# A two-layer graph attention and expert kernel: the rows of five pairs fetched and normalized during layer 0's last expert blocks, and one ring of single-row buffers beside attention 1

## The chip, the cores and the metric

The kernel runs on one core of a Trainium2 chip. The core has a tensor engine (PE, with a second row PEld for its weight loads), a vector engine (DVE), a scalar engine (ACT), a general engine (POOL) and SyncE (SP), whose queue issues most of the DMAs here. All of them work through their own instructions in order and wait for one another with semaphores. The metric is the time of one execution in microseconds on the device, lower is better. Line numbers (L1444) are those of the kernel before.

## The reference

N = 2708 nodes with 256 features, and a 0/1 adjacency matrix of 2708 x 2708. Two layers, each a graph attention and a sparse mixture of experts, with residuals:

```python
# layer 0
x = x + gnn0(layernorm(x), adj)       # h = x W^T; softmax over neighbours of leaky_relu(s_i + s_j); att @ h
x = x + ffn0(layernorm(x))            # 8 experts, top 2, 256 -> 1024 -> 256, erf gelu
# layer 1
x = x + gnn1(layernorm(x), adj)       # hyperbolic: logmap, W_gcn, expmap/logmap, W_att, masked softmax,
                                      # elu, proj, logmap, sigmoid, expmap
x = x + ffn1(layernorm(x))            # 16 experts, top 2, 256 -> 512 -> 256, relu, then y = layernorm(x + moe)
```

All data is float32. What matters here is the seam between the two layers: attention 1 of any node needs `layernorm(x)` of all nodes, where x is the finished output of layer 0, and its projection `u = layernorm(x) @ w1x` (two weight matrices of 256 x 256 side by side, so 512 columns) must be there for all nodes before any row of attention 1 can be summed.

## The kernel before

**Tiles.** The nodes are cut into T = 22 tiles of up to 128 rows (20 full ones and two of 74 rows), taken as 11 pairs. `x_all` holds x of all tiles while layer 0's attention runs; `h_all` holds 22 x 257 values per partition in layer 1.

**Layer 0's experts.** The router scatters every node's row (twice, top 2) to pages of 128 rows per expert in DRAM (`rows_d`). 47 sure blocks and three that run only if needed (`rest`, behind a branch at L929) then go through `Experts.run`: for block b, SP loads W1 and W2 of its expert (1 MB each, L743 and L747) two blocks ahead into one of three rooms, and fetches the 128 rows three blocks ahead (L759). PE multiplies `hid_ps` (L874), ACT applies gelu with the table loaded for it (L878), PE multiplies `out_ps` of the block before (L892), DVE scales it (L898, after `side` at L866 and the weight `w`, ACT L868), and POOL adds the rows with an indirect DMA into one of two sums in DRAM, `sums0[0]` for even blocks and `sums0[1]` for odd ones (L903). `sums0[0]` begins with x, so x of layer 1 is `sums0[0] + sums0[1]`. A hook `beside(b)` is called in every block after its row fetch.

**The seam.** After the branch of `rest`, ACT loads another table (L1418). Then `project1` is started for one pair after another by `Turns`, a list of generators that are stepped round by round: this only writes down the order of instructions on each engine; the engines then run as their waits allow. A pair goes through: two fetches of 256 KB from the sums (L1444), POOL's sum of the two (L1468), a store of the sum to `x_d` in DRAM (L1455), DVE's mean and variance (L421, L422), ACT's Ln and Exp for the deviation (L428, L429), one Newton step on DVE (L374), two normalizations (L437) into tiles `xr`, four transposes on PE (L455), ACT's copy `xts` (L1491) and sums of squares (L1496), eight matmuls `u_ps` (L460), and for each tile a sum of squares and a copy to `h_all` on ACT (L1505, L1507). The fetch of the first pair has to wait until the last add of layer 0 has landed, and the PE has nothing else to do. `factors1` then makes the softmax factors, `split_h` the two halves of h, and attention 1 begins (L1570). POOL widens the masks (L1430, two of them ahead of the first pair; ACT widens two, L1432).

**Attention 1 and layer 1's experts** are ordered by a planner: generators tell what engine they want and for how long, and `Clock` and `Slots` order them. `points1` closes a group of six tiles: it fetches its x back from `x_d`, three pairs into the ring `xp` of four pair buffers (`xps`, four slots), combines them on DVE (L1778), normalizes on ACT and gives the rows to the router. The same SP queue then carries the weights and rows of layer 1's experts.

**Buffers.** Pools stand on one another in SBUF; a pool that is opened where another was closed makes its first writer wait for the last reader there.

**DMA semaphores.** The built program gives SP's transfers eight semaphores in turn, so a transfer is issued only once the one eight places ahead of it has landed.

Of the kernel before, what the change touches and what calls it, by code (L numbers as in the profile page):

```python
# [22 lines left out]
P = 128  # L23
# [123 lines left out]
def kernel(  # L147
# [72 lines left out]
    def row_tile(name, bufs):  # L220
        return row.tile([P, D], F32, name=name, tag=name, bufs=bufs)
# [26 lines left out]

    room_scope = ExitStack()
# [6 lines left out]
    def xn_tile():  # L256
        return keep0.tile([P, RW], F32, name="xn", bufs=4)
# [16 lines left out]

    x_all = keep0.tile([P, T, D], F32, name="x_all")
# [431 lines left out]
    class Experts:  # L707
# [5 lines left out]
        def __init__(self, layer, router, w1, b1, w2, func, sums, tags, xg, xt, bias, sure):  # L713
            self.layer, self.router, self.w1, self.w2 = layer, router, w1, w2
            self.func, self.sums, self.b1 = func, sums, b1
            self.t_tag, self.h_tag, self.o_tag = tags
            self.xg_tile, self.xt_tile, self.bias_tile = xg, xt, bias
            E, _, self.F = w1.shape
            self.FC, self.NB = self.F // P, router.blocks
            self.rooms, self.rows, self.known, self.planned, self.stages = {}, {}, 0, 0, []  # L720
            self.last_add, self.adds = {}, []
            self.b1_rows = w1x.rearrange("p c f -> p (c f)")[:E, :self.F]
            self.taken, self.sure = taken_of[layer], sure
# [177 lines left out]
        def add(self, b, yo):  # L901
            k = b % 2
            ins = nc.gpsimd.indirect_dma_start(  # L903
                out=self.sums[k][:, :], in_=yo, in_offset=None,
                out_offset=bass.IndirectOffsetOnAxis(ap=self.rows.pop(b)[:, D:D + 1].bitcast(I32),
                                                     axis=0), compute_op=OP.add)
            if k in self.last_add:
                tc.add_manual_dep(ins.ins, self.last_add[k].name, LANDED, reason="the same rows")
            self.last_add[k] = ins.ins
            if k == 0:  # L910
                self.adds.append(ins.ins)
# [6 lines left out]
        def store(self, t, r, src):  # L918

            ins = nc.sync.dma_start(self.sums[0][t * P:t * P + r, :], src)  # L920
            for other in self.adds:
                tc.declare_no_dep(ins.ins, other, reason="other tokens' rows")

# [306 lines left out]
    def close0(pair, ahead, behind, last=False):  # L1230
# [19 lines left out]
        for t, r in pair:  # L1250
            router0.rows[t] = keep0.tile([P, RW], F32, name="xr", bufs=5)
            ln_f0.apply(router0.rows[t][:r, :D], x_all[:r, t, :], t, r)
            yield 1
# [137 lines left out]

    with tc.tile_pool(name="experts0", bufs=1) as late0:
        room = late0.tile([P, 4096], F32, name="room2")
        experts0.add_room(2, room[:, :2048], room[:, 2048:])
        l1_weights = []

        def combine(b):
            if b == EARLY0 + 2:
                l1_weights.extend(load_combined(late0))
            if b == EARLY0 + 4:  # L1400
                combine_weights(*l1_weights)

        experts0.run(late0, turns, (2, 1, 2), combine)
# [6 lines left out]
    h_all = side.tile([P, T, D + 1], F32, name="h_all1")  # L1410
# [24 lines left out]
    ln_a1 = Norm("a1")  # L1435
    c0, scale, p_all, p_scale = kept("c0", 1.0), kept("scale"), kept("p_all"), kept("p_scale")
    norms = kept("norms", 1.0, 2 * T).rearrange("p (k t) -> p k t", k=2)

    def fetch_rows(tl, src, group):

        full = [t for t, r in group if r == P]
        if full:
            lo = full[0] * P
            nc.sync.dma_start(tl[:, :len(full)], src[lo:lo + len(full) * P, :].rearrange(  # L1444
                "(t p) d -> p t d", p=P))
        if len(full) < len(group):
            nc.sync.dma_start(tl[:TAIL, len(full):], src[TF * P:W, :].rearrange(
                "(t p) d -> p t d", p=P)[:TAIL])

    x_d = dram.tile([W, D], F32, name="x_d")  # L1450

    def keep_rows(src, pair):
        if pair[1][1] == P:
            lo = pair[0][0] * P
            nc.sync.dma_start(x_d[lo:lo + 2 * P, :].rearrange("(t p) d -> p t d", p=P), src)  # L1455
        else:
            for q, (t, r) in enumerate(pair):
                nc.sync.dma_start(x_d[t * P:t * P + r, :], src[:r, q])

    def project1(pair):  # L1460

        xa = h_all[:, pair[0][0]:pair[0][0] + 2, :D]
        xb = side.tile([P, 2, D], F32, name="xp", bufs=4)
        fetch_rows(xa, sums0[0], pair)
        fetch_rows(xb, sums0[1], pair)
        yield 3
        if pair[1][1] == P:
            nc.gpsimd.tensor_tensor(xa, xa, xb, OP.add)  # L1468
        else:
            for q, (t, r) in enumerate(pair):  # L1470
                nc.gpsimd.tensor_tensor(xa[:r, q], xa[:r, q], xb[:r, q], OP.add)
# [8 lines left out]
        xp = [side.tile([P, RW], F32, name="xr", bufs=13)[:, :D] for _ in pair]  # L1480
        for q, (t, r) in enumerate(pair):
            ln_a1.apply(xp[q][:r], xa[:r, q], t, r)
        yield 1
        ps = ps_tile("tr_ps", "tr").rearrange("p (t c n) -> p t c n", c=DC, n=P)
# [10 lines left out]
        for q, (t, r) in enumerate(pair):  # L1495
            nc.scalar.activation(row_tile("junk", 4)[:r, 1:], xp[q][:r, 1:], AF.Square,  # L1496
                                 accum_out=norms[:r, 0, t:t + 1])
# [83 lines left out]
    widen(0, 1)  # L1581
    widen(1, 1)
    FIRST = 12
    for k in range(len(pairs) + 11):
        if k < len(pairs):
            turns.start(project1(pairs[k]))
        turns.step()
        if k in (12, 14):
            widen(k // 2 - 6, 0)

        if k == FIRST // 2 + 10:
            turns.start(factors1(0, FIRST))
        if k >= FIRST // 2 + 13:
            lo = 4 * (k - FIRST // 2 - 13)
            split_h(lo, lo + 4)
# [24 lines left out]
    def xr_tile():  # L1620
        return side.tile([P, RW], F32, name="xr", bufs=13)

# [13 lines left out]
    bank, acc, xrs, xps, los, xtss = (Slots(clock, n) for n in (5, 3, 13, 4, 2, 2))  # L1636
# [48 lines left out]
    def finish1(t, r):  # L1685
# [3 lines left out]
        lo, ex = (side.tile([P, D], F32, name=nm, bufs=2) for nm in ("lo", "ex"))  # L1689
# [35 lines left out]
    def points1(group):  # L1725
# [5 lines left out]
        def fetch_x():  # L1731
            for k in range(0, n, 2):
                xp_slots.append((yield from xps.get()))
                xp = side.tile([P, 2, D], F32, name="xp", bufs=4)
                fetch_rows(xp, x_d, group[k:k + 2])
                xq.extend((xp[:, 0], xp[:, 1]))
                clock.moved(x_at[k // 2], 0.9, 2.0)
# [36 lines left out]
        for q, (t, r) in enumerate(group):  # L1774
            if q % 2 == 0:
                yield x_at[q // 2]
            yield "DVE", 1.1
            nc.vector.scalar_tensor_tensor(x1[:r, t, :], emb[:r, t, :], by[:r, q:q + 1], xq[q][:r],  # L1778
                                           op0=OP.mult, op1=OP.add)
            ln_f1.stats(x1[:r, t, :], t, r)  # L1780
            if q % 2:
                clock.set(xp_slots[q // 2])
# [183 lines left out]
```

## Time and profile before

| | us |
|---|---|
| median of 9 runs (1185.93 to 1192.27) | 1190.67 |
| the profiled execution, its own time | 1186.91 |
| its span | 1185.2 |
| around the span | 1.7 |

The profiled execution lies 3.8 us below the median. Sums in the prediction are made in the profiled execution and then moved to the median.

| engine | busy us | share of the span |
|---|---|---|
| PE | 1058.1 | 89% |
| PEld | 936.8 | 79% |
| ACT | 585.7 | 49% |
| DVE | 526.4 | 44% |
| POOL | 404.0 | 34% |

In order of time: layer 0's projections (to about 50 us), its attention and router (to 306), its experts (306 to 669), the seam with the projections of layer 1 (669 to 733), attention 1 (733 to 891), layer 1's experts (911 to 1133), and the end (to 1185). A timeline line gives the start, the time from the first start to the last end of the merged instructions, the engine and the instructions, and in brackets the idle time before them with what ended it. A line of windows gives the stretch, and for each engine its busy time and count, the clock granted to the PE, the share of the DMA engines' time, and GB/s. A line of waits gives who waited for whom: us in total, times, the longest.

### The profile page before, as it was taken

Reading aid. Unit: us, or ns where it says so; the run is one execution under the profiler, and the core shown is the slowest. Engines: PE = TensorE matmul, PEld = TensorE weight load, DVE = VectorE, ACT = ScalarE, POOL = GpSimd, SP = SyncE. Lnnn points to the kernel's source line nnn. Section 1 sums busy time; section 2 is a strip of 40 time slices with the busy share of each in tenths; the row PEclk is TensorE's granted clock in tenths of the full one; section 3 lists DMA queues with packets and bytes.
Section 4 is the critical chain, followed back from the end, with each engine's and each line's share of the span. In section 5 each row is a group of like instructions: output and inputs, shape, how many; then the busy total and the mean of one; then the engine's idle time right before and its main releaser. Section 6 shows DMA issues by size and latency. Waiting matters only on the chain. (4 is left out here: it accounts for less than half of the span.)

```text
span 1185.2 us, 21436 instructions
## 1 busy us (share of the span) xinstructions
PE 1058.1 (89%) x6753; PEld 936.8 (79%) x6753; DVE 526.4 (44%) x2024; ACT 585.7 (49%) x1637; POOL 404.0 (34%) x467
## 2 busy tenths in 40 slices
PE   5999999969989999999999589998993878999963
PEld 4888888857879999989999545998983767898852
DVE  7778888856421111110111175458765641111136
ACT  4876676644524444434444276546562333444413
POOL 7621121111242222221222340443644455384325
PEclk9999999998999999999999889998986789999987
DMA  9953444311879999999899579001114367787963
GB/s 303 315 204 136 173 154 159 135 72 62 302 231 314 322 322 321 327 291 321 270 320 325 137 257 323 25 1 54 55 63 163 107 188 175 178 212 187 259 191 110
DMA packets 163486, 238.96 MB, mean 202 GB/s; under 512 B 10415, under 2 KB 137046, under 8 KB 160658
## 3 DMA queue, kind: packets, MB, share of 16 engines
q1 hardware_dynamic: 144550, 214.09, 54.3%
q0 software_dynamic: 18816, 23.42, 10.2%
q8 instruction: 57, 0.93, 0.3%
q14 instruction: 63, 0.52, 0.1%
HBM read 205.54 MB, written 54.99 MB: 220 GB/s over the span
## 5 line engine op out<-in xcount | busy, mean ns | idle before, releaser
L898 DVE TENSOR_SCALAR yo<-out_ps,w 128x256 f32<-128x256 f32 x92 | 44.5, 484 | 430.9 <-PE out_ps L892 423.7
L1219 PE MATMUL att_ps<-g_all,z 128*128 128x257 f32 (+3 forms) x968 | 226.0, 386 | 0.5 <-DVE z L1208 0.5
L1219 PEld LDWEIGHTS att_ps<-g_all,z 128*128 128x128 f32 (+3 forms) x968 | 176.0, 187 | 37.4 <-issue 9.4
L892 PE MATMUL out_ps<-room,ht 128*128 128x256 f32 x872 | 200.6, 382 | 0.0
L874 PEld LDWEIGHTS hid_ps<-xt,room 128*128 128x128 f32 x1504 | 175.6, 192 | 6.1 <-issue 3.1
L874 PE MATMUL hid_ps<-xt,room 128*128 128x128 f32 x1504 | 177.2, 276 | 3.3 <-issue 2.7
L892 PEld LDWEIGHTS out_ps<-room,ht 128*128 128x128 f32 x872 | 162.4, 192 | 21.0
L1205 ACT ACTIVATE zr<-e_bc,minus_one,g_all 128x256 f32<-128x256 f32 (+3 forms) x242 | 130.6, 591 | 55.0 <-DVE z L1208 54.3
L903 POOL DMA_INDIRECT sums<-yo,xg x43 | 66.9, 1557 | 244.5 <-DVE side L866 196.1
L878 ACT ACTIVATE ht<-hid_ps,w_t 128x128 f32<-128x128 f32 x376 | 127.9, 364 | 27.1 <-PE hid_ps L874 5.7
L668 POOL DMA_INDIRECT rows_d<-xr,place x88 | 91.7, 1042 | 126.0 <-DVE xr L437 77.0
L1570 PE MATMUL att_ps<-half,wide_mask 128*128 128x258 f32 (+1 forms) x968 | 128.0, 295 | 3.6 <-issue 2.1
L1570 PEld LDWEIGHTS att_ps<-half,wide_mask 128*128 128x128 f32 (+1 forms) x968 | 124.5, 199 | 5.3 <-issue 2.8
L1208 DVE SCALAR_TENSOR_TENSOR z<-zr,mask_t 128x256 f32<-128x256 f32 (+3 forms) x242 | 98.6, 428 | 34.1 <-ACT zr L1205 18.9
L878 ACT ACTIVATE ht<-hid_ps,w1x 128x128 f32<-128x128 f32 x180 | 65.0, 364 | 94.1 <-PE hid_ps L874 69.0
L903 POOL DMA_INDIRECT sums<-yo,xr x45 | 70.1, 1558 | 87.3 <-DVE w L896 40.2
L868 ACT ACTIVATE w<-xg,side 128x1 f32<-128x1 f32 x43 | 12.7, 295 | 165.9 <-DVE side L866 165.9
L455 PE MATMUL tr_ps<-ident,xr 128*128 128x128 f32 (+1 forms) x222 | 41.5, 298 | 35.8 <-DVE xr L437 16.0
L1430 POOL CAST wide_mask<-mask_t 128x1408 fp32r<-128x1408 fp8e4 x31 | 42.5, 1376 | 85.4 <-PE att_ps L1570 85.4
L874 PE MATMUL hid_ps<-lo,wide_mask 128*128 128x128 f32 x480 | 65.9, 294 | 2.6 <-DMA wide_mask<-in_L_ffn_w_dram 2.6
L874 PEld LDWEIGHTS hid_ps<-lo,wide_mask 128*128 128x128 f32 x480 | 62.9, 207 | 6.1 <-issue 5.0
L455 PEld LDWEIGHTS tr_ps<-ident,xr 128*128 128x128 f32 (+1 forms) x222 | 29.7, 156 | 44.0 <-issue 18.6
(287 smaller groups left out, 1437.7 us busy)
## 6 DMA issues: line engine op xcount, KB each, us to landing
room<-in_L_ffn_W_dram SPq DMA_DIRECT2D x94, 1024.0 KB
wide_mask<-in_L_ffn_w_dram SPq DMA_DIRECT2D x60, 512.0 KB
room<-in_adj_dram SPq DMA_DIRECT2D x20, 1354.0 KB
room<-in_L_ffn_w_dram SPq DMA_DIRECT2D x30, 512.0 KB
rows_d<-nobody SPq DMA_DIRECT2D x1, 7511.0 KB
rows_d<-nobody SPq DMA_DIRECT2D x5, 1295.0 KB
sums<-nobody SPq DMA_DIRECT2D x2, 2944.0 KB
xr<-rows_d SPq DMA_DIRECT2D x45, 129.5 KB
```

What stands on the lines that cost most here:

```text
L455: nc.tensor.transpose(ps[:, c, :r], src[:, c * P:(c + 1) * P], ident[:r, :r])
L668: ins = nc.gpsimd.indirect_dma_start(out=self.rows_d[:, :], in_=self.rows[t][:r], in_offset=None, out_offset=bass.IndirectOffsetOnAxis(ap= ...
L874: nc.tensor.matmul(ps[:, :P], w1_b[:, c, f * P:(f + 1) * P], xt[:, c, :], start=(c == 0), stop=(c == DC - 1))
L878: nc.scalar.activation(ht[:, f, :], ps[:, :P], self.func, bias=self.bias[:, f, b:b + 1])
L892: nc.tensor.matmul(ps[:, :D], ht[:, f, :], self.rooms[b % 3][1][:, f, :], start=False, stop=(f == self.FC - 1))
L898: nc.vector.tensor_scalar(yo, ps[:, :D], w, None, op0=OP.mult)
L903: ins = nc.gpsimd.indirect_dma_start(out=self.sums[k][:, :], in_=yo, in_offset=None, out_offset=bass.IndirectOffsetOnAxis(ap=self.rows.pop ...
L1205: nc.scalar.activation(zr[:k, :n], e_bc[:k, lo:lo + n], AF.Relu, bias=minus_one[:k], scale=g_all[:k, j, D + 1:D + 2])
L1208: nc.vector.scalar_tensor_tensor(z[:k, :n], zr[:k, :n], 1.0, mask_t[:k, j // 2, lo:lo + n, j % 2], op0=OP.add, op1=OP.mult)
L1219: nc.tensor.matmul(accs[i][:r, :D + 1], z[:k, q * P:q * P + r], g_all[:k, j, :D + 1], start=(j == 0), stop=(j == LAST))
L1430: nc.gpsimd.tensor_copy(m, src)
L1570: nc.tensor.matmul(accs[i][:, :D + 2], wide_masks[i, j % 2][:k, j // 2, :], half_k[:k, j, :], start=(j == 0 and half_k is halves[0]), stop ...
```

## The change

Ten tiles (five pairs) of layer 1's x are fetched before layer 0 is done. The hook `ahead(b)` of the expert blocks fetches both sums of pairs 0 to 2 in block 40 and of pairs 3 and 4 in block 41 on SP, and POOL adds them; DVE takes mean and variance in blocks 43 and 44; in block 45 DVE makes all ten deviations, SP stores the five pairs to `x_d`, and DVE normalizes four of the pairs; in block 46 ACT takes the sums of squares of these four. By the router's paging these nodes' rows all lie in the first 32 blocks, so `early_read` frees the fetches from waiting for later adds. After the branch, `project1` of pairs 0 to 4 begins with the transposes; the other six pairs go through `prepare1`, with `sums0[1]` fetched row tile by row tile.

The buffers: `x_all` and `h_all` become one tile of 257 columns in a pool that lasts (`lasting`), as do `xn` (four) and `xr` (five). The pair ring `xp` of layer 1 is gone: in the seam its rows go to the ring `xr1` of 13, and `points1` fetches its x one tile at a time into the five `xr`, with `xps` at two pair slots. `finish1` takes `xn` for `ex`. The four first mask widenings move behind the seventh round of the seam.

```diff
+    lasting = mask_scope.enter_context(tc.tile_pool(name="lasting", bufs=1))
+    h_all = lasting.tile([P, T, D + 1], F32, name="h_all")
+    x_all = h_all[:, :, :D]
...
     def xn_tile():
-        return keep0.tile([P, RW], F32, name="xn", bufs=4)
+        return lasting.tile([P, RW], F32, name="xn", bufs=4)
+    def xr0_tile():
+        return lasting.tile([P, RW], F32, name="xr", bufs=5)
...
+        def early_read(self, k, ins, done):
+            for b, other in self.adds[k]:
+                if b >= done:
+                    tc.declare_no_dep(ins.ins, other, reason="other tokens' rows")
+            self.early_reads[k].append(ins.ins)
...
+    AHEAD = 5
+    MOST, DONE = 4 * AHEAD + E0 - 1, EARLY0 + E0
...
+    def square_rows(xp, pair):
+        for q, (t, r) in enumerate(pair):
+            nc.scalar.activation(row_tile("junk", 4)[:r, 1:], xp[q][:r, 1:], AF.Square,
+                                 accum_out=norms[:r, 0, t:t + 1])
+
+    def ahead(b):
+        left = SURE0 - 1 - b
+        if left in (6, 5):
+            for k in range(3) if left == 6 else range(3, AHEAD):
+                for half, at in ((0, 2 * k), (1, at2 + 2 * k)):
+                    experts0.early_read(half, fetch_rows(h_all[:, at:at + 2, :D], sums0[half],
+                                                         pairs[k]), DONE)
+                xa = h_all[:, 2 * k:2 * k + 2, :D]
+                nc.gpsimd.tensor_tensor(xa, xa, h_all[:, at2 + 2 * k:at2 + 2 * k + 2, :D], OP.add)
+        if left in (3, 2):
+            for t, r in first[:6] if left == 3 else first[6:]:
+                ln_a1.stats(x_all[:, t], t, r)
+        if left == 1:
+            rsqrt(ts(ln_a1.mv[:, :2 * AHEAD, 1], LN_EPS, OP.add), ln_a1.rstd[:, :2 * AHEAD])
+            for k, pair in enumerate(pairs[:AHEAD]):
+                keep_rows(h_all[:, 2 * k:2 * k + 2, :D], pair)
+                if k < AHEAD - 1:
+                    normed[k] = [(xn_tile if k < 2 else xr0_tile)()[:, :D] for _ in pair]
+                    for xp, (t, r) in zip(normed[k], pair):
+                        ln_a1.apply(xp, x_all[:, t], t, r)
+        if left == 0:
+            for k, pair in enumerate(pairs[:AHEAD - 1]):
+                square_rows(normed[k], pair)
...
+            ahead(b)
...
-    def project1(pair):
+    def xr_tile():
+        return side.tile([P, RW], F32, name="xr1", bufs=13)
+    def fetch_row(tl, src, t, r):
+        nc.sync.dma_start(tl[:r], src[t * P:t * P + r, :])
+    def prepare1(pair):
         xa = h_all[:, pair[0][0]:pair[0][0] + 2, :D]
-        xb = side.tile([P, 2, D], F32, name="xp", bufs=4)
+        xb = [xr_tile()[:, :D] for _ in pair]
         fetch_rows(xa, sums0[0], pair)
-        fetch_rows(xb, sums0[1], pair)
+        for q, (t, r) in enumerate(pair):
+            fetch_row(xb[q], sums0[1], t, r)
         yield 3
...
+        yield from project1(pair, xp)
+    def project1(pair, xp):
...
+        if pairs.index(pair) >= AHEAD - 1:
+            square_rows(xp, pair)
...
-    widen(0, 1)
-    widen(1, 1)
     FIRST = 12
-    for k in range(len(pairs) + 11):
-        if k < len(pairs):
-            turns.start(project1(pairs[k]))
+    last = pairs[AHEAD - 1]
+    normed[AHEAD - 1] = [xr_tile()[:, :D] for _ in last]
+    for xp, (t, r) in zip(normed[AHEAD - 1], last):
+        ln_a1.apply(xp, x_all[:, t], t, r)
+    for k in range(AHEAD):
+        turns.start(project1(pairs[k], normed[k]), k)
+    for k in range(17):
+        if AHEAD + k < len(pairs):
+            turns.start(prepare1(pairs[AHEAD + k]))
         turns.step()
-        if k in (12, 14):
-            widen(k // 2 - 6, 0)
+        if 6 <= k < 10:
+            widen(k % 2, k < 8)
...
-    bank, acc, xrs, xps, los, xtss = (Slots(clock, n) for n in (5, 3, 13, 4, 2, 2))
+    bank, acc, xrs, xps, los, xtss = (Slots(clock, n) for n in (5, 3, 13, 2, 2, 2))
...
-        lo, ex = (side.tile([P, D], F32, name=nm, bufs=2) for nm in ("lo", "ex"))
+        lo, ex = side.tile([P, D], F32, name="lo", bufs=2), xn_tile()[:, :D]
...
-                xp = side.tile([P, 2, D], F32, name="xp", bufs=4)
-                fetch_rows(xp, x_d, group[k:k + 2])
-                xq.extend((xp[:, 0], xp[:, 1]))
+                for t, r in group[k:k + 2]:
+                    xq.append(xr0_tile())
+                    fetch_row(xq[-1][:, :D], x_d, t, r)
                 clock.moved(x_at[k // 2], 0.9, 2.0)
```

## The prediction

> **What bounds the kernel now.** I read the windows by stage, then the timeline of the seam engine by engine, then the lists of waits. The windows: while layer 0's experts run, the PE is never idle and the DMA engines are full too; in the seam the PE stands for 14.9 us; then it is full again.
>
> ```profile
> 620.00:640.00 20.00, 20.00 (x145) 18.98 (x144) 2.27 (x9) 9.39 (x30) 4.66 (x3) 1.00 1.01 328
> ...
> 657.00:668.60 11.60, 11.60 (x71) 10.24 (x69) 1.52 (x6) 4.47 (x11) 3.11 (x2) 1.00 0.18 25
> 668.60:683.50 14.90, 0.03 (x1) 0.02 (x1) 4.22 (x15) 1.00 (x4) 8.66 (x10) 0.63 0.72 210
> 683.50:691.50 8.00, 6.87 (x17) 3.64 (x18) 7.44 (x30) 4.68 (x19) 5.15 (x12) 0.63 1.09 382
> 691.50:722.00 30.50, 30.50 (x96) 15.11 (x95) 16.04 (x65) 26.42 (x104) 9.02 (x20) 1.00 0.78 230
> ```
>
> The columns are PE, PEld, DVE, ACT, POOL, clock, DMA share, GB/s. The reader is to see two resources that are full before the seam, and only one (PE) that is full after it. The PE's timeline:
>
> ```profile
> 665.02 3.62 PE L892 MATMUL out_ps<-room,ht 128*128 128x256 f32 x16
> 683.51 1.09 PE L455 MATMUL tr_ps<-ident,xr 128*128 128x128 f32 x4 [14.88 <-DVE xr L437]
> ...
> 686.63 4.99 PE L460 MATMUL u_ps<-w1x,xts 128*128 128x512 f32 x8
> ...
> 691.90 3.60 PE L460 MATMUL u_ps<-w1x,xts 128*128 128x512 f32 x8
> ...
> 695.77 3.60 PE L460 MATMUL u_ps<-w1x,xts 128*128 128x512 f32 x8
> ...
> 732.70 6.03 PE L1570 MATMUL att_ps<-half,wide_mask 128*128 128x258 f32 x48 [1.53 <-ACT h_all L1507]
> ```
>
> Layer 0 ends at 668.64. The first projection is 18.0 us later, and from there the pairs follow every 3.87 us (691.90 to 695.77) to the start of attention 1. Why the first one is late, on ACT and SP:
>
> ```profile
> 665.75 0.29 ACT L868 ACTIVATE w<-xg,side 128x1 f32<-128x1 f32 x1 [3.84 <-DVE side L866]
> 666.53 1.28 ACT L1418 ACT_TABLE_LOAD   x1 [0.49 <-ACTq L929]
> ...
> 673.35 0.39 SPq L1444 DMA_DIRECT2D h_all<-sums  x1
> ```
>
> The last add lands, the fetch leaves at 673.35, POOL begins its sum at 677.06, and mean, deviation and normalization end at 683.5: a chain of latencies. The weights of the last blocks, from SP's timeline, and later the waits of PE where layer 1's experts begin:
>
> ```profile
> 646.32 0.37 SPq L743 DMA_DIRECT2D room<-in_L_ffn_W_dram  x1
> 650.60 0.37 SPq L747 DMA_DIRECT2D room<-in_L_ffn_W_dram  x1
> ```
> ```profile
> PE tr_ps L455 <- DMA xr<-rows_d: 8.1, 1, 8.1
> PE tr_ps L455 <- ACT w1x L850: 6.1, 1, 6.1
> ```
>
> The last 1 MB of W1 (L743) is used at 657.76, the last W2 at 665.02; the DMA engines fall silent at 657 (share 0.18 after it).
>
> **The change, part by part.**
>
> *The first projection.* Pairs 0 to 3 are normalized before the branch, so their transposes need only the end of `out_ps`. What is late next is ACT: block 46's weight `w` ends at 666.04, and behind it now stand eight sums of squares. A pair of them took 685.54 to 686.45, 0.91 us, so 4 x 0.91 = 3.6 us, to 669.7; 0.49 of branch and 1.28 of table load (rows above) to 671.4; `xts` 0.57; and 0.98 from its end to the first matmul (685.65 to 686.63): 673.0. PE has its two pairs of transposes (1.1 us each) done by 670.9. The projection starts at 673.0 instead of 686.63: **-13.6 us**. Bounds: -13.6 - 1.8 if the table load lies under other work, and -10 if the squares cost twice.
>
> After that the PE sets the pace, as between 691.5 and 722. ACT has less to do for the first pairs (no squares, no Ln and Exp), and was 26.42 of 30.50 busy.
>
> *Pair 5,* the first that is fetched late. Its fetch leaves when the last add has landed, 673.35 as before, and before it took from there to 683.5 until normalized; with the PE at 673.0 + 5 x 3.87 = 692.4 only then in need of it, 8.9 us of cover. But in the order written out, projections 3 and 4 stand together and pair 5's transposes come after both: then transposes 0.6, ACT's rest of projection 4 (0.57 + 0.36), `xts` 0.6, and the start. Between 0 (ACT is ahead) and 2.7 us; I take **+1.5**, nearer the longer since each link has a row.
>
> *The ten fetches in blocks 40 and 41.* They stand on SP's queue ahead of W1 of blocks 43 and 44, where the DMA engines are full (1.01). 10 x 262 KB; the same transfers ran in the seam at 382 GB/s (row 683.5:691.5), so 6.9 us of DMA time, and all later weights are that much later. What they can lose: the last W2 began 1.05 MB / 328 GB/s = 3.2 us before the silence at 657, so the last W1 had landed by about 653.8 and was used at 657.76: 4.0 us. 6.9 - 4.0 = 2.9 us of standing PE: **+3.0**. Bounds: 0 if the stage has slack that the share hides, 6.9 if W1 has none. With eight transfers open at most, W1 of block 43 also waits on SP until W2 of block 42 has landed; the fetches ahead of it keep the engines busy meanwhile, so this costs nothing more. W2 has 8 us and is covered.
>
> *The rest of the early work* costs nothing. POOL's five adds (1.18 us each) and the small copies lie between its row adds, before each of which it idles 5.6 us or more; if that cover went, the row add would be late, with four `yo` buffers behind it. DVE's ten means and variances (0.6 each, blocks 43 and 44) and 12 small steps of 0.2 with eight normalizations of 0.37 (5.4 us in block 45) go into idle times of 6.0 us before each `yo`. The five `x_d` stores leave after the last W2, into the silence of 657 to 668.6; behind them SP has only the branch. POOL's two widenings (2.66 us) leave a place where POOL waited for a transfer anyway, and 18 fetches instead of 12 for the six late pairs, 0.5 us each on SP, go beside 23 us of projections.
>
> *The start.* x now lands in rows of 257, in pieces of 1 KB instead of 2 KB. PE and DVE wait for one such transfer there (3.56 us for the first). One takes 262 KB / 382 GB/s = 0.7 us, so between 0 and 0.7, **+0.4**.
>
> *Layer 1's x.* The third pair of a group can be fetched only when the first is used. For the first two groups there are more than 4 us on DVE between them. For the third group, two fetches now stand on SP ahead of the first row gather: 2 x 0.45, **+0.9**, since the PE waits 8.1 us for that gather. Their landing behind 2.1 MB of weights (6.4 us at 328 GB/s) would put the group's router late; DVE then does other groups' work. 0 to 5.6 us for each of two groups; I take 0, as the PE has planned blocks to run.
>
> Sum: -13.6 + 1.5 + 3.0 + 0.4 + 0.9 = **-7.8 us**: 1179.1 in terms of the profiled execution (1186.91, span 1185.2 and 1.7 around it), which lies 3.8 under the median of 1190.67; so **1182.9** for the median.
>
> [...] In this trace, idle times of 14.88 and 3.85 us (812.65 to 816.50) are followed by a clock below full, 0.63 in the stretch 683.5 to 691.5, and the first projection took 5.27 to the second instead of 3.87: 1.4 us. I let the changed kernel pay the same 1.4, as its idle time of some 2 to 4 us with transposes in it is nearer the 3.85 than nothing. [...]
>
> **The rivals.**
> - *The weights take it back.* If the fetches run at half the seam's rate against the full stage, they cost 13.8 us of queue, less 4.0: +9.8 in place of 3.0, sum -1.0, median 1189.7. For it: 1.01 of share with no idle stretch. Against: the same transfers reach 382 GB/s beside others.
> - *Slower: the ring of five in layer 1.* If the third pair's late x delays the routers of the third and fourth group by 5.6 us each and the in-order PE stands at their gates, that is +11.2: sum +3.4, median 1194.1. It decides from 10.2 us on. For it: PE's waits there (8.1, 6.1) are for just such things. Against: up to eight blocks of 3.85 us are planned by then.
> - *Hidden anyway.* Attention 1 starts no earlier, since something beside the projections sets it: about 1190 with the costs kept small. Against: its last wait was 1.53 us for ACT `h_all`, the projections' own end.
>
> **How the numbers follow.** Forecast 0.70, all of it faster; weights 0.13 (0.05 still faster, 0.08 within); ring 0.14 (0.12 slower, 0.02 within); hidden 0.03, within, of which 0.01 I give to slower. A measurement of this kernel tells about 0.2% (2.4 us) from no change: faster 0.75, same 0.12, slower 0.13. The forecast's own bounds: the costs all at zero with the table load covered give -15.4, and stall 6.9 with bubble 2.7, start 0.7 and gather 0.9 give -2.4; median 1175.3 to 1188.3. The range reaches on to the ring: 1175 to 1194.
>
> **What would show it.** Right: PE's wait at the first transposes under 2 us; first projection about 4.4 us after layer 0's last `out_ps` (18.0 before) and behind ACT's table load; attention 1 some 8 us earlier; in blocks 43 to 46 waits of `hid_ps` for `room` of about 3 us in sum. Wrong: waits for `room` of 7 us or more; the gap from the end of attention 1 to the first `hid_ps` of layer 1 (890.2 to 912.6 now) grown by more than 3 us, or the one from there to the experts' end (1132).

## The result, and the profile after

| | us |
|---|---|
| kernel before, median of 27 runs (1185.93 to 1196.87) | 1192.06 |
| changed kernel, median of 9 runs (1180.62 to 1184.69) | 1181.77 |
| ratio, with its 95% interval | 0.9918 (0.9897 to 0.9938) |
| profiled execution of the changed kernel, own time and span | 1183.41, 1181.5 |

The change makes the kernel 0.6 to 1.0% faster. The predicted 1182.9 lies 1.1 us from the median; as a difference, -7.8 us stood against -9.8 by the ratio. That it came so near is in part luck: the sum missed 2.7 us of gain in the seam (-12.1 predicted, -14.8 measured) and 2 to 4 us of cost in layers 0 and 1, and the two nearly cancel. The windows of the changed kernel, over the same stretches as before; the columns are again PE, PEld, DVE, ACT, POOL, clock, DMA share and GB/s:

```profile
620.00:640.00 20.00, 17.98 (x127) 16.67 (x126) 2.27 (x9) 7.78 (x25) 8.46 (x6) 1.00 1.06 345
640.00:657.00 17.00, 14.67 (x88) 13.48 (x87) 3.63 (x15) 5.56 (x16) 4.62 (x4) 0.90 1.07 367
657.00:668.60 11.60, 11.60 (x89) 11.07 (x88) 6.39 (x29) 6.07 (x19) 3.71 (x4) 1.00 0.85 242
668.60:683.50 14.90, 13.25 (x56) 8.95 (x55) 3.92 (x12) 7.80 (x27) 8.24 (x15) 1.00 0.31 66
```

Where PE stood for 14.9 us, it is now busy for 13.25. But PE is no longer full from 620 to 657, and this is new. Its timeline shows both:

```profile
637.90 3.81 PE L880 MATMUL hid_ps<-xt,room 128*128 128x128 f32 x32 [2.02 <-DMA room<-in_L_ffn_W_dram]
...
647.82 5.43 PE L880 MATMUL hid_ps<-xt,room 128*128 128x128 f32 x32 [2.33 <-DMA room<-in_L_ffn_W_dram]
...
671.48 3.62 PE L898 MATMUL out_ps<-room,ht 128*128 128x256 f32 x16
676.16 1.06 PE L461 MATMUL tr_ps<-ident,xn 128*128 128x128 f32 x8 [1.07 <-DVEq L943]
677.81 3.67 PE L466 MATMUL u_ps<-w1x,xts 128*128 128x512 f32 x8 [0.59 <-ACT xts L1555]
681.76 3.60 PE L466 MATMUL u_ps<-w1x,xts 128*128 128x512 f32 x8
...
698.27 3.70 PE L466 MATMUL u_ps<-w1x,xts 128*128 128x512 f32 x8 [0.86 <-ACT xts L1555]
...
724.35 6.03 PE L1633 MATMUL att_ps<-half,wide_mask 128*128 128x258 f32 x48 [1.53 <-ACT h_all L1570]
```

In blocks 43 and 44 PE waits for W1, 4.35 us in sum, and block 44's `hid_ps` takes 5.43 us instead of 3.81. Layer 0's last `out_ps` starts at 671.48, 6.46 us later than the 665.02 of before. From there the first projection is 6.33 us away (21.61 before), and attention 1 starts at 724.35 instead of 732.70. Why W1 is late, on SP's timeline:

```profile
622.81 5.00 SPq L1415 DMA_DIRECT2D h_all<-sums  x6
629.34 0.38 SPq L749 DMA_DIRECT2D room<-in_L_ffn_W_dram  x1
633.89 3.81 SPq L1415 DMA_DIRECT2D h_all<-sums  x4
639.22 0.38 SPq L749 DMA_DIRECT2D room<-in_L_ffn_W_dram  x1
```

The six fetches of block 40 hold SP for 5.00 us. W1 of block 43 leaves at 629.34, 5.1 us later than before (624.26), and is used 8.56 us after its issue. In the kernel before 11.44 us lay between issue and use (624.26 to 635.70), so 2.9 us of the delay were covered and about 2 were not.

The stages of all kernels, each from the start of one instruction to that of another in the kernel's own timeline. *Last blocks*: from the `out_ps` of block 35 to that of block 46 (its first row, with the bias). *Seam*: from the last `out_ps` to attention 1. *Behind attention*: from the first `where_ps` at the end of attention 1 to layer 1's first `hid_ps`. *Layer 1's experts*: from there to their last `out_ps`.

| kernel | last blocks | seam | behind attention | layer 1's experts |
|---|---|---|---|---|
| before | 76.91 | 67.68 | 21.85 | 218.31 |
| changed | 83.37 | 52.87 | 23.69 | 219.42 |
| changed, again (e5) | 81.30 | 52.92 | 24.03 | 220.86 |
| e1, e6: one pair per block | 77.25, 76.91 | 52.89, 52.87 | 23.22, 24.41 | 225.38, 218.93 |
| e2: fetches by ACT | 86.17 | 52.90 | 23.75 | 219.22 |
| e3: three pairs | 78.43 | 58.39 | 23.96 | 227.04 |
| e4: before, two slots | 76.90 | 67.60 | 23.74 | 218.34 |
| e7: e1 and four slots | 79.03 | 52.79 | 23.15 | 222.28 |
| e8: e7 and shift | 77.79 | 52.12 | 22.63 | 219.93 |
| e11: merged fetches | 81.61 | 52.88 | 23.85 | 223.12 |
| e12: e8, factors earlier, every second block | 76.91 | 49.44 | 22.63 | 223.49 |
| e9: e8, factors and halves earlier, every second block (faster chip) | 76.91 | 53.45 | 17.61 | 209.51 |
| e10: fetches by POOL (faster chip) | 76.91 | 52.89 | 18.10 | 215.08 |

e9 and e10 ran on a chip on which the kernel before is faster too (1170.62); there is no profile of it from there, so their last two columns have nothing to stand beside. For the other rows, the first three columns repeat within about 2 us in the kernels that share the part. The last one does not: one and the same kernel took 225.38 and 218.93 (e1, e6). Nor do two stretches outside the table: the time up to block 35 (588.0 before, 587.5 to 592.7 in all) and attention 1 itself (158.1 before, 160.2 and 158.0 in two executions of the changed kernel, 156.7 to 162.7 in all). So the profiled execution of the changed kernel is only 3.5 us shorter than that of before, while its first three columns add up to -6.5. Single profiled executions are compared by stage here, and whole times only by their ratios.

### The profile page after: what moved, and what is told of

It reads as the page before. It is cut to its first block, busy times and chain, and to the rows that moved or that the text cites. A ratio compares the mean times of both kernels' runs of the same rounds, so it can differ in the third digit from the quotient of the medians.

```text
span 1181.5 us, 21452 instructions
## 1 busy us (share of the span) xinstructions
PE 1053.1 (89%) x6753; PEld 931.8 (79%) x6753; DVE 523.9 (44%) x2021; ACT 584.8 (49%) x1627; POOL 404.6 (34%) x472
## 5 line engine op out<-in xcount | busy, mean ns | idle before, releaser
L884 ACT ACTIVATE ht<-hid_ps,w_t 128x128 f32<-128x128 f32 x376 | 128.6, 365 | 33.2 <-PE hid_ps L880 12.1
L461 PE MATMUL tr_ps<-ident,xr 128*128 128x128 f32 (+1 forms) x214 | 38.0, 285 | 23.7 <-DMA xr<-rows_d 8.7
L898 PE MATMUL out_ps<-wide_mask,ht 128*128 128x256 f32 x240 | 58.4, 387 | 0.0
```

The source lines that it names most:

```text
L461: nc.tensor.transpose(ps[:, c, :r], src[:, c * P:(c + 1) * P], ident[:r, :r])
L884: nc.scalar.activation(ht[:, f, :], ps[:, :P], self.func, bias=self.bias[:, f, b:b + 1])
L898: nc.tensor.matmul(ps[:, :D], ht[:, f, :], self.rooms[b % 3][1][:, f, :], start=False, stop=(f == self.FC - 1))
```

## The experiments

**The order of the early fetches (e1, e6).** The fetches leave one pair per block, in blocks 35 to 39.

```diff
-        if left in (6, 5):
-            for k in range(3) if left == 6 else range(3, AHEAD):
+        if 7 <= left < 7 + AHEAD:
+            for k in (6 + AHEAD - left,):
```

> The changed kernel with the ten early fetches one pair per block in blocks 35 to 39, instead of three pairs in block 40 and two in block 41. Burst theory: layer 0 ended 6.46 us later in the changed kernel (675.10 against 668.64) because 2.6 MB came at once in front of two weights; one pair per block is 0.52 MB, 1.4 us at 382 GB/s, under the 4 us by which W1 lands early, so no wait for room in blocks 40 to 46, layer 0 ends within 0.7 us of 668.6, and the kernel gains 5 to 6 us on the changed one (about 1176 beside a before of 1192). Volume theory: the DMA engines are full all along, so the same bytes cost the same wherever they stand: waits for room of about 4 us in sum, only in earlier blocks, and the time stays that of the changed kernel. Given-back theory: layer 0 ends 6 us earlier, but what stands behind attention 1 takes it back, and the whole gains less than 2 us.

Measured: ratio 0.9918 (0.9890 to 0.9947). No wait for room; last blocks 77.25 against 83.37, attention 1 at 719.17, 5.2 us before the changed kernel's 724.35. The windows show PE busy for 36.90 of 37 us where the changed kernel has 32.65:

```profile
620.00:640.00 20.00, 19.90 (x140) 18.49 (x139) 2.28 (x9) 8.54 (x27) 6.46 (x5) 1.00 1.08 369
640.00:657.00 17.00, 17.00 (x119) 15.97 (x118) 6.27 (x26) 7.54 (x24) 3.10 (x2) 1.00 1.03 333
```

The burst theory holds for the place, and the volume theory falls. But by the ratio the whole had not gained: 0.9918, as for the changed kernel, which was not measured beside it here; and the profiled execution took 225.38 us in layer 1's experts. So both kernels went once more, side by side.

> The changed kernel once more, as it is, beside the spread one. If the seam's gain reaches the end whole: 8.35 us (the earlier start of attention 1) less the 2 us that the order of layer 1 costs, ratio to before about 0.9947. If the first measurement (0.9918) holds, 2 to 4 us more come from somewhere that the first two profiles do not show. The first profile's part from the first hid_ps of layer 1 to the experts' last out_ps was 219.4 us and that of the spread kernel 225.4; if that part varies from execution to execution it will be another number here, between 218 and 227.

> The kernel with one early pair per block in blocks 35 to 39, once more, beside the changed kernel on the same chip. Burst theory with nothing given back: 4 to 6 us faster than the changed kernel of this comparison. Given-back theory: within 2 us of it, and then its time from the first hid_ps of layer 1 to the experts' last out_ps is again some 225 us where the changed kernel has 219; with nothing given back that time is as long in one as in the other, apart from single executions.

Measured: 0.9923 (0.9898 to 0.9949) for the changed kernel, 0.9884 (0.9858 to 0.9911) for the spread one; medians 1186.58 and 1183.05. By the medians the spread kernel is 3.5 us faster, a little under the 4 to 6 expected; the intervals of the two ratios overlap, and the first comparison saw no difference, so the gain in the whole time is less firm than that in the last blocks. Its layer 1 took 218.93 us this time: the long one of e1 does not belong to the kernel, and the given-back theory falls. The 4.4 us of this second execution of the changed kernel are again waits for room:

```profile
641.37 3.81 PE L880 MATMUL hid_ps<-xt,room 128*128 128x128 f32 x32 [2.32 <-DMA room<-in_L_ffn_W_dram]
650.55 3.81 PE L880 MATMUL hid_ps<-xt,room 128*128 128x128 f32 x32 [1.59 <-DMA room<-in_L_ffn_W_dram]
```

They are 3.91 us, 0.4 less than in the first profile, and both `hid_ps` took 3.81 us. Of the 2.1 us between the two executions the other 1.6 are the slow `hid_ps` of the first, at a clock of 0.50 (last section).

**Fewer pairs (e3).** `AHEAD = 3` instead of 5, and the loop of the seam two rounds longer (`range(19)`, `split_h` from round 16).

> The changed kernel with AHEAD 3 instead of 5: six early fetches in block 40, none in 41, eight pairs late. Burst theory: 1.57 MB are 4.1 us at 382 GB/s and 4.9 at 322, against 4 us by which W1 lands early: 0 to 1 us of waits for room, layer 0 ends 0 to 1 us later than 668.6, so 5.5 to 6.5 us are gained there. In the seam the first late pair is wanted 14.4 us after layer 0's end (2.7 and three pairs of 3.87) and can be projected about 17.8 after it (fetch 4.6 after, 10.2 to normalized, 3 to the first matmul): 3.4 us of standing PE where the changed kernel had 1.7. Together 4 to 5 us faster than the changed kernel. If the late weights had another cause than the number of bytes, layer 0 still ends near 675 and the kernel is 1 to 2 us slower than the changed one.

Measured: 0.9950 (0.9921 to 0.9979). One wait for room of 1.29 us; last blocks 78.43, 1.5 us longer than before. So 1.57 MB cost 1.5 us and 2.62 MB 4.4 to 6.5: a fixed reserve is used up first, as the burst theory has it. The seam lost more than expected: PE stood 2.35 and 2.30 us for the late pairs, the next projection ran at a lower clock (0.70 from 695.2 to 700.5, and 5.16 instead of 3.60 us), and the seam took 58.39, 5.5 us more than with five pairs instead of 1.7. Three pairs are too few; four were not tried.

**Bytes or number of transfers (e2, e10, e11).** In the trace of the changed kernel SP's 462 transfers carry eight semaphores in turn, 57 or 58 each, and up to the seam each shares one with the transfer eight places ahead. For W1 of block 43 that is W2 of block 42: W1 left at 629.34, 0.23 us after the last landing update of this W2 (629.11). Was W1 late by the bytes, or by its place behind ten transfers? The first trial lets ACT issue them (`queue=nc.scalar` in `fetch_rows`, for the early fetches alone).

> The changed kernel with the ten early fetches issued by ACT instead of SP, in the same blocks 40 and 41. Bandwidth theory: the bytes go through the same DMA engines, so W1 of blocks 43 and 44 is as late as before: waits for room of 4 to 5 us in sum, layer 0 ends at about 675, time as the changed kernel's within 1.5 us. Queue theory: W1 was late because it stood on SP behind ten transfers, each to be issued only after the one eight places ahead had landed; from ACT's queue the fetches pass beside it, waits for room fall under 1 us and layer 0 ends at about 669; ten issues on ACT of some 0.4 us are hidden. Then 5 us faster than the changed kernel.

Measured: 0.9952 (0.9918 to 0.9986). The waits for room are gone, but PE waits for ACT instead. The list of PE's waits from 600 to 660, then ACT's own issues from its timeline:

```profile
PE hid_ps L880 <- ACT ht L884: 5.4, 2, 3.4
```

```profile
621.32 3.96 ACTq L1415 DMA_DIRECT2D h_all<-sums  x6
633.98 2.64 ACTq L1415 DMA_DIRECT2D h_all<-sums  x4
```

Ten issues took 6.6 us of ACT, 0.66 each, and gelu (`ht`) stood behind them; the last blocks took 86.17. As PE was late itself, it could no longer see whether W1 was: the trial does not decide. Nor did it take the fetches out of SP's way. From SP's own list of waits in the same stretch:

```profile
SPq L753 <- DMA h_all<-sums: 8.0, 1, 8.0
```

SP stood 8.0 us ahead of W2 of block 42 until a fetch of ACT had landed, and W1 of block 43 left at 628.93, nearly as late as in the changed kernel (629.34). The second trial lets POOL issue them (`nc.gpsimd`).

> The changed kernel with the ten early fetches in blocks 40 and 41 issued by POOL, which stands idle 5.6 us or more before each of its row adds, instead of by SP; the engine whose delay spoilt the trial with ACT's queue is left alone. Bandwidth theory: the bytes are the same and the DMA engines full, so PE still waits 3.5 to 4.5 us for room in blocks 43 and 44 and layer 0's last part is 4 to 7 us longer than the 135.6 of before. Queue theory: the weights' place behind the fetches on SP was the cause: waits for room under 1 us in sum, the last part within 1 us of 135.6, and 4 us or more faster than the changed kernel.

Measured: 0.9910 (0.9877 to 0.9943), on another chip, where the kernel before took 1170.62 us. It does not decide either. The ten fetches did not stay in blocks 40 and 41; the first and the last of them in POOL's timeline:

```profile
81.19 0.77 POOL L1415 DMA_DIRECT2D h_all<-sums  x1 [12.13 <-DVE xr L443]
...
317.84 0.75 POOL L1415 DMA_DIRECT2D h_all<-sums  x1 [8.66 <-DMA sums<-h_all]
```

They stood in POOL's order ahead of the experts' adds, the first of which is at 326. So in this kernel ten tiles of layer 1 go on from x without layer 0's expert outputs, which is another computation. It only shows the last blocks with nothing fetched beside them: 76.91. The third trial leaves the fetches on SP and merges them:

```diff
+            lo, hi = (0, 3) if left == 6 else (3, AHEAD)
+            for half, at in ((0, 0), (1, at2)):
+                experts0.early_read(half, fetch_rows(
+                    h_all[:, at + 2 * lo:at + 2 * hi, :D], sums0[half], tiles[2 * lo:2 * hi]), DONE)
```

> The changed kernel with the ten early fetches merged into four: in block 40 one transfer of six tiles from each sum, in block 41 one of four tiles from each; the same bytes at the same place on SP, six issues less. Byte theory: the waits for room stay at 3.5 to 4.5 us in sum (4.35 and 3.91 in the two profiles of the changed kernel), and layer 0's last part (w_ps to the last out_ps, 135.6 us in the kernel before) stays 4 to 7 us longer. Count theory: what made W1 late is the number of transfers on SP, each issued only when the one eight places ahead had landed; with four instead of ten the waits fall under 1.5 us and the last part is at most 1.5 us longer than before.

Measured: 0.9907 (0.9875 to 0.9939). The last blocks took 81.61, 4.7 us more than before and within what ten transfers cost (4.4 and 6.5). The waits for room, one of 2.54 us with a slow `hid_ps` behind it, lie between the two theories:

```profile
638.63 5.43 PE L880 MATMUL hid_ps<-xt,room 128*128 128x128 f32 x32 [2.54 <-DMA room<-in_L_ffn_W_dram]
```

The sum of the waits fell from 3.9 or more to 2.5 us, but not because W1 came earlier. The first wait is no shorter behind two transfers than behind six (2.54 against 2.02 and 2.32), although W1 left SP at 628.38, 1 us earlier than in the changed kernel. The second W1 landed at 647.8 by the semaphore updates in the trace, against 647.7 in the changed kernel; PE came to it only at 647.9, since the slow `hid_ps` had cost it 1.6 us, and so did not wait. So it is the bytes that come at once, and not the number of transfers, as far as one execution tells.

**The ring in layer 1 (e4, e7).** In e4 the kernel before gets the two slots alone; in e7 the spread kernel gets four again, with the pairs taking rows from `xr` and `xn` in turn, `ex` in buffers of its own, and `junk` cut to two buffers to make room.

```diff
-    bank, acc, xrs, xps, los, xtss = (Slots(clock, n) for n in (5, 3, 13, 4, 2, 2))
+    bank, acc, xrs, xps, los, xtss = (Slots(clock, n) for n in (5, 3, 13, 2, 2, 2))
```

> The kernel before with the planner's pair slots for layer 1's x cut from four to two (the buffers stay): the third part of the change alone, without the early fetches. My prediction's theory: the PE's order behind attention 1 moves (fewer transposes together, blocks earlier), the first hid_ps of layer 1 comes 0 to 2 us later after the end of attention 1 than the 22.1 us of before, and the time is within 2 us of before. Ring theory: the routers of the third and fourth group come late, the gap grows by 3 us or more, and the kernel is 5 to 11 us slower than before. Gain theory: part of the changed kernel's gain is the new order in layer 1 (its median lies 10 us below, its profiled seam only 8): then this alone is 2 to 4 us faster than before.

> The spread kernel, and layer 1's x with four pair slots again, as in the kernel before (rows from the rings xr and xn in turn, ex in buffers of its own, junk cut to two to make room). Ring theory: the two slots cost 2 us, by the PE's order behind attention 1, so this is 2 us faster than the spread kernel, with the gap from the last att_ps to the first hid_ps back from 23.7 to about 22 us. Rival: the order makes no difference that lasts; within 1 us.

Measured: 1.0015 (0.9994 to 1.0037) for e4. Behind attention 1 it takes 23.74 instead of 21.85 us: 1.9 us, and nothing of the 5 to 11 us of the ring theory. The waits of the kernel before, and then those of e4, in the same stretch (885 to 920):

```profile
PE bias_ps L845 <- issue: 9.9, 1, 9.9
PE tr_ps L455 <- DMA xr<-rows_d: 8.1, 1, 8.1
```
```profile
PE bias_ps L845 <- DVE hot_f L837: 11.4, 1, 11.4
PE tr_ps L455 <- DMA xr<-rows_d: 8.8, 1, 8.8
```

Both waits that were there are longer, by 1.5 and 0.7 us. With four slots in e7 the part is 23.15, in e8 and e12 22.63, against 23.22 and 24.41 in the two executions of the spread kernel: some of the loss seems to come back, but two executions of one kernel differ as much. The ratio of e7, 0.9876 (0.9847 to 0.9905), cannot be told from the spread kernel's 0.9884. What makes DVE late for `hot_f` in the new order stays open.

**The order in the seam (e8, e9, e12).** Pair 5 stood for ACT's `xts`. In e8 the early pairs start one round later, and a late pair's transposes follow its normalization in the same round.

```diff
-        turns.start(project1(pairs[k], normed[k]), k)
+        turns.start(project1(pairs[k], normed[k]), k + 1)
...
-        yield 1
         yield from project1(pair, xp)
```

> As the one before, and in the seam the early pairs start one round later and a late pair's transposes follow its normalization in the same round, so that pair 5's copy xts stands on ACT ahead of pair 4's copies to h_all. Order theory: the standing of 1.7 us at pair 5 goes, attention 1 starts 1.5 us earlier after layer 0's end (52.9 from the last out_ps's start in the changed kernel), and the time is 1 to 1.5 us shorter. Rival: pair 5 is late by its fetch, not by order: the stall stays, or moves to the Ln and Exp of the late pairs on ACT, and the time is within 1 us or longer.

Measured: 0.9883 (0.9856 to 0.9910). The stall goes: every pair now follows after 3.87 us. But attention 1 starts only 0.7 us earlier, because something else is late next, in PE's timeline:

```profile
695.53 3.60 PE L466 MATMUL u_ps<-w1x,xts 128*128 128x512 f32 x8
699.40 3.60 PE L466 MATMUL u_ps<-w1x,xts 128*128 128x512 f32 x8
...
721.88 7.93 PE L1632 MATMUL att_ps<-half,wide_mask 128*128 128x258 f32 x48 [3.96 <-ACT half L1618]
```

The halves wait for 6.8 us of DVE steps of `factors1`, which begin at 713. So e9 starts `factors1` and `split_h` two rounds earlier, and fetches one pair in every second block, since e7 and e8 had lost 2.1 and 0.9 us in the last blocks, 1.3 and 0.5 of it in small waits of `hid_ps` for ACT's `w` and for W1.

```diff
-        if 7 <= left < 7 + AHEAD:
-            for k in (6 + AHEAD - left,):
+        if left in (12, 10, 8, 6, 4):
+            for k in ((12 - left) // 2,):
...
-        if k == FIRST // 2 - AHEAD + 10:
+        if k == FIRST // 2 - AHEAD + 8:
```

> The kernel with four slots and the shifted seam, with factors1 and split_h of the first six pairs two rounds earlier, and one early pair in every second block (34, 36, 38, 40, 42) instead of every block. What was seen: with the shift the projections run through without a stall, but attention 1 waits 3.96 us for the halves, behind 6.8 us of DVE steps of factors1 that begin at 713. Theory: started 7 us earlier they end before the last projection; the wait falls under 1.5 us, attention 1 begins 48 to 50 us after the last out_ps of layer 0 (52.1 before this edit), and the kernel is 2 to 4 us faster than the shifted one. Rival: the first halves are now on ACT ahead of the last pairs' copies, the last projections wait for them, and attention 1 begins within 1 us of where it did. For the fetches: with 14.7 us between two pairs no wait for room over 0.3 us, and layer 0's last part as long as before (135.6 us from w_ps to the last out_ps).

Measured: 0.9866 (0.9839 to 0.9893), on the chip of e10. The last blocks are 76.91, as before. The rival came true in kind for the seam: 53.45 us, 1.3 more than with the shift alone. It is not the halves that stand in the way, but `p_all`: ACT comes to it too early, and what stands behind it holds the last projections. The ratio cannot be told from e8's.

```profile
708.66 0.21 ACT L1596 ACTIVATE p_all<-stat 128x12 f32<-128x12 f32 x1 [5.15 <-DVE stat L375]
```
```profile
709.55 6.80 PE L466 MATMUL u_ps<-w1x,xts 128*128 128x512 f32 x12 [2.76 <-ACT h_all L1569]
```

In e12 `split_h` stands where it stood, and a round lies between the DVE steps and `p_all`:

```diff
+        yield 1
         nc.scalar.activation(p_all[:, lo:hi], score, AF.Exp)
```

> The kernel with four slots and the shifted seam, one early pair in every second block, factors1 two rounds earlier, but its Exp of p_all one round behind the DVE steps before it and split_h where it stood. Seen in the trial with factors1 earlier: ACT came to p_all 5.15 us before DVE had its input, and h_all of the eighth and ninth pair, which stand behind it, held the last projections back by 2.76 us. Theory: with p_all one round later the last projections run through, attention 1 begins 49 to 50.5 us after layer 0's last out_ps (53.45 there, 52.1 with the shift alone, 52.9 in the changed kernel), and no wait for room over 0.3 us: 13 to 16 us faster than before by the seam, less up to 1 us in layer 1. Rival: the wait moves to another place of the same chain and attention 1 begins at 52 us or later; then no faster than the spread kernel, ratio about 0.988.

Measured: 0.9857 (0.9829 to 0.9884), median 1175.40 against 1191.29 of before. `p_all` waits 1.92 us instead of 5.15, attention 1 starts 49.44 us after the last `out_ps`, and no wait for room is left:

```profile
709.93 0.21 ACT L1597 ACTIVATE p_all<-stat 128x12 f32<-128x12 f32 x1 [1.92 <-DVE stat L375]
```
```profile
706.12 7.08 PE L466 MATMUL u_ps<-w1x,xts 128*128 128x512 f32 x16
714.48 6.42 PE L1633 MATMUL att_ps<-half,wide_mask 128*128 128x258 f32 x48 [1.29 <-ACT half L1619]
```

This is the best kernel of the study, 15.9 us faster than before by the medians, 17.0 by the ratio. The theory held for the place. "13 to 16 us" was met in the medians, though the seam alone is 18.2 us shorter (67.68 to 49.44); against the spread kernel's 0.9884 the intervals overlap, so that step is shown in the seam (3.4 us) and not yet in the whole time.

## Why the prediction was right

The forecast was right in its mechanism: faster, by the seam, with the price paid in layer 0 and a little in layer 1. That the sum came within 2 us is in part luck, since its misses have opposite signs. By its own steps:

- *The first projection, -13.6: right, and too small.* From the last `out_ps` it came 15.3 us earlier (21.61 to 6.33). It starts 2.7 us after layer 0's end, not 4.4, and behind ACT's table load as told. The largest piece is the 0.98 from the end of `xts` to the first matmul: in the kernel before PE was at the transposes of the second pair in that time (from 685.72, 1.11 us), and now they are done and it is 0.14. ACT's eight squares follow every 0.40 us, 3.3 instead of 3.6 us in all, and the table load follows 0.1 us after them: the 0.49 of branch that stood in the row of before is no longer seen.

```profile
675.20 0.40 ACT L1443 ACTIVATE junk<-xr 128x255 f32<-128x255 f32 x1
675.50 0.18 ACT L1443 ACTIVATION_READ_ACCUMULATOR junk<-xr 128x1 f32 x1
675.79 1.28 ACT L1498 ACT_TABLE_LOAD   x1
677.08 1.07 ACT L1555 COPY xts<-tr_ps 128x512 f32<-128x512 f32 x2
```

- *The clock, no change: wrong by 1.3 us in favour.* The first two projections are 3.95 us apart (677.81 to 681.76), not 5.27, and 3.94 to 3.95 in every kernel with early pairs; the clock was 1.00 from 668.6 to 691.5. Without the 1.4 us that the prediction let the changed kernel pay, its sum is -9.2. The row that was nearest (a wait of 3.85 us) was the wrong neighbour for two waits of 1.07 and 0.59.
- *Pair 5, +1.5: right.* The rest of the seam, from the first projection to attention 1, grew by 0.5 us (46.07 to 46.54) although the clock gave 1.3: 1.8 us of stalls. e8 shows that they are the order on ACT, as the step said, and not the late fetch.
- *The ten fetches, +3.0: the step that failed most.* They cost 6.46 us in the first profile and 4.4 in the second. The step took 6.9 us of transfers less 4.0 of slack. In blocks 43 and 44 the waits are 3.9 to 4.35, so that 2.5 to 3.0 us of the 6.9 were covered; e3 says the same (4.1 us of transfers, 1.29 of wait, 2.8 covered). The 4.0 was worked out from a rate (the last W1 landed by about 653.8), and it was not there even in the kernel before: by the semaphore updates in its trace the last piece of that W1 landed at 655.36 or later, at most 2.4 us ahead of its use, and those of W1 of blocks 43 and 44 at most 3.5 and 3.4 us ahead. On top came 1.6 us of clock in the first execution, which the step did not have. The bounds of 0 to 6.9 held.
- *The start, +0.4:* not seen. PE's first transposes begin at 9.94 us in both kernels.
- *Layer 1's x, +0.9 with 0 for the routers: right in kind, half in size.* About 1.9 us behind attention 1 (e4), no more anywhere that repeats. The wait for the first row gather, which the step named, grew by 0.6 to 0.7 us (8.1 to 8.7 in the changed kernel, 8.8 in e4); the rest is the wait of `bias_ps`, which it did not name.
- *The early work at nothing: right.* In the changed kernel every wait of PE in the last blocks is for W1.

The sum by stages is -14.8 + 4.4 to 6.5 + 1.9, so -6.4 to -8.5, against -7.8 predicted. The two measured ratios are -9.8 and -9.2 us, with intervals that begin at -7.4 and -6.1. Whether 1 to 3 us more come from a place that changes from execution to execution (attention 1 and layer 1's experts do) stays open.

The rivals: of "the weights take it back" about half the price came, 4.4 to 6.5 us instead of 9.8; whether the fetches ran at half the seam's rate is not shown. "Slower" fell with e4. "Hidden anyway" fell with attention 1 at 724.35.

## What to carry to other kernels

Work that is moved under a stage whose DMA engines are already full (a share of 1.01 here) should be cut into pieces smaller than the margin of one step: the same 2.62 MB cost 4.4 to 6.5 us in two blocks, and 0 to 2.1 us one pair per block, and nothing in every second block. Read such a margin from the landing of the loads in the blocks where the new transfers will run, and not from a mean rate at the end of the stage. And when a stall has been taken out of a chain of engines in order, look for the next one before counting the gain: here it was `factors1`, then the place of one Exp on ACT.

## What was not expected of the hardware

The clock fell after waits shorter than the 14.88 and 3.85 us of the prediction's rows. PE stood from 645.5 to 647.8, and the next 3.4 us ran at half the clock:

```profile
645.50:647.80 2.30, 0.00 (x0) 0.01 (x1) 2.17 (x9) 0.29 (x1) 2.08 (x3) 1.00 1.09 363
647.80:651.20 3.40, 3.38 (x16) 3.40 (x17) 1.46 (x7) 1.10 (x3) 0.26 (x1) 0.50 1.05 396
651.20:654.00 2.80, 2.80 (x24) 2.73 (x24) 0.00 (x0) 2.10 (x6) 0.00 (x0) 1.00 1.17 324
```

The same happened after 2.54 us in e11 (0.50 from 638.6 to 642.0). In the second execution of the changed kernel a wait of 2.32 us was followed by full clock:

```profile
641.30:644.70 3.40, 3.33 (x30) 3.36 (x31) 0.00 (x0) 2.21 (x6) 1.40 (x2) 1.00 1.10 371
```

So waits of 2.3 us sometimes cost another 1.6 us and sometimes nothing. The kernel before has a case as well: 0.50 from 334.44 to 337.86, after idle times of 1.99 and 0.75 us. What decides it the traces do not show.

The second surprise is how long a queue is held by its issues. A late fetch of a pair in the seam took SP 0.37 to 0.47 us, hardly more than a weight load (0.37). The same fetch took 0.83 where six stood together beside full DMA engines (a share of 1.06; 5.00 for six), and 0.66 on ACT's queue there (6.6 us for ten), with gelu behind them. What holds the queue in that time the traces do not show.
